# A state-space scan on one core: one product with C for three blocks, carried states by DMA and through the matmul, and the diagonal form of B throughout

## The chip, the cores and the metric

The kernel runs on one core of one Trainium2 chip. The metric is device time in microseconds (us), as the median of several runs. A core has a TensorE (PE; its weight loads are shown on a row of their own, PEld), a VectorE (DVE), a ScalarE (ACT) and a GpSimd (POOL); SyncE (SP) issues most of the transfers here. Each engine works through its own queue in order.

## The reference

Four layers follow each other on eight images of 64 x 64 positions and 192 channels. The change touches only the core of layer 1, a selective scan over L = 4096 positions in four directions k (along rows, along columns, and both backwards), with 384 channels and N = 16 states a channel:

```python
x_hwwh = jnp.stack([x_flat, x_trans], axis=1)
xs = jnp.concatenate([x_hwwh, jnp.flip(x_hwwh, axis=-1)], axis=1)
x_dbl = jnp.einsum('bkdl,kcd->bkcl', xs, x_proj_weight)
dts, Bs, Cs = jnp.split(x_dbl, [R, R + N], axis=2)
dts = jnp.einsum('bkrl,kdr->bkdl', dts, dt_projs_weight)
A = -jnp.exp(A_logs).reshape(4, Din, N)
delta = jax.nn.softplus(dts + dt_projs_bias[None, :, :, None])

def step(h, inp):
    u_l, d_l, B_l, C_l = inp
    dA = jnp.exp(d_l[..., None] * A)
    dBu = d_l[..., None] * B_l[:, :, None, :] * u_l[..., None]
    h = dA * h + dBu
    y = jnp.sum(h * C_l[:, :, None, :], axis=-1)
    return (h, y)
```

So for each channel and each state n: a decay dA that depends on the position, an input d·B·u, the recurrence h = dA·h + dBu, and a sum over n of h·C.

## The kernel before

The program runs layer 0, the input part of layer 1 (projection, convolution), the scan (`layer1_scan`), and a tail with the rest. Each is a stage; the scan's stage does not overlap the others.

The scan is cut into 256 *steps*: image b, direction k, piece p of 512 positions (NJ). For k >= 2 pieces and positions are walked backwards. The first piece of each (b, k) starts from zero, so 7 steps of 8 take over a state from the step before. A step has 16 *groups* (one for each state n, called g over the whole stage), and a group three *blocks* o of 128 channels (j counts blocks; 12288 in all). For one block:

- `ahead(j)`: ACT makes the decay `dA` (128 channels x 512 positions) as an exponential of `dl` times a scalar for each channel. PE makes the input `pd` in PSUM, in four squares of 128x128. The product of step size and input lies in `dut` with positions on partitions; it must be multiplied by B, one number for each position, and turned over. Two forms do this, by turns. For even g (`diagonal`) ACT makes a diagonal matrix `bd` of B (the identity times a scalar for each partition), and PE multiplies `dut` with it (L1009). For odd g ACT multiplies all 384 columns of `dut` by B into `sb`, and PE transposes that (L1011).
- `scan(j)`: DVE runs the recurrence over 512 positions with one instruction (L1044), with the start taken from `st`, the last column of the same state in the step before. POOL multiplies the block with C (`bc`, the row of C on all partitions, brought by a transfer, L993) into `hc` (L1053). After the third block POOL copies the three last columns into `st` (L1055).
- `behind(j)`: PE transposes `hc` in four squares and adds them up over n in PSUM, in `yt` (L942, `add_rows`). After the last n, `take` copies `yt` out with ACT, and a transfer writes it.

`prepare` readies the next step's `dl` and `dut`: transposes (L888, L922), three products (L901), exponentials and logarithms on ACT, and sums and products on DVE. Its pieces are spread over the positions of the current step by the list `at`.

On PE, DVE, ACT and POOL the order is the one written in the program: for each j, in turn, `fetch(g + 2)` (once a group), `ahead(j + 2)`, `scale(g + 2)` (makes `bd` or `sb`), `scan(j)`, `behind(j - 2)`, and what `todo` holds of `prepare`. SP's order is set by a scheduler. Buffers: `dA` 5, `pd` 3, `h` 2 (of three blocks each), `hc` 6 (of one block), `bc` 4, `bd` 10, `sb` 8. All data are f32.

Of the kernel before, what the change touches and what calls it, by code (L numbers as in the profile page):

```python
# [10 lines left out]
AF = mybir.ActivationFunctionType  # L11
ALU = mybir.AluOpType
# [6 lines left out]
DIN = 384  # L19
DP, DT = 128, 3  # L20
NH, HD, NS = 6, 64, 64
N1, R1, K1 = 16, 12, 4
# [3 lines left out]
NJ = 512  # L26
# [3 lines left out]
class Names:  # L30
    n = 0


def mk(pool, shape, tag, **kw):
    Names.n += 1
    return pool.tile(shape, F32, tag=tag, name=f"{tag}_{Names.n}", **kw)
# [795 lines left out]
def layer1_scan(ctx: ExitStack, tc, a, load, ur, ut, xd, yk, cst):  # L832

    nc = tc.nc
    ident = cst[0]
    wp = ctx.enter_context(tc.tile_pool(name="ws1", bufs=1))
    w_dt = load("w_dt", [1 + R1, K1, DIN])
    aneg = load("A_logs", [DP, K1, DT, N1])
    ds = load("Ds", [DP, K1, DT])
    nc.scalar.activation(aneg, aneg, AF.Exp)  # L840
    nc.vector.tensor_scalar(aneg, aneg, -1.0, None, ALU.mult)
    dsum = mk(wp, [DP, DT], "dsum")
    nc.vector.tensor_tensor(dsum, ds[:, 0, :], ds[:, 1, :], ALU.add)
    for k in range(2, K1):
# [5 lines left out]
    pp = ctx.enter_context(tc.tile_pool(name="p1", bufs=2))  # L850
# [17 lines left out]
    steps = []  # L868
# [2 lines left out]
            order = range(NCH) if k < 2 else range(NCH - 1, -1, -1)  # L871
            steps += [(b, k, p, i == 0) for i, p in enumerate(order)]

    def prepare(b, k, p, made):


        def fetch_rows():
            made["xt"] = mk(pp, [128, NB, c], "xt")
            made["dut"] = mk(pp, [128, NB, DIN], "dut")
            for q, v in by_piece(xd[b][:, k, :], k, p):  # L880
                nc.sync.dma_start(made["xt"][q], v)
            for q, v in by_piece(ut[b], k, p):
                nc.sync.dma_start(made["dut"][q], v)

        def turn_xd():
            ps = made["ps"] = mk(psum, [128, NJ], "mm")[:c]
            for t in range(NB):
                nc.tensor.transpose(ps[:, t * 128 : (t + 1) * 128], made["xt"][:, t, :], ident)  # L888

        def turned_xd():  # L890
            xs = made["xs"] = mk(pp, [c, NJ], "xs", bufs=1)
            nc.scalar.copy(xs, made.pop("ps"))
            bcd = made["bcd"] = mk(dram, [N1, NJ], "bcd")
            nc.sync.dma_start(bcd, xs[1 + R1 + N1 :, :])
            made["e"] = mk(pp, [DP, DT, NJ], "e", bufs=1)
            made["dl"] = mk(pp, [DP, DT, NJ], "dl")


        def step_mm(o):
            ps = made["ps", o] = mk(psum, [128, NJ], "mm")  # L900
            nc.tensor.matmul(  # L901
                ps, w_dt[:, k, o * 128 : (o + 1) * 128], made["xs"][0 : 1 + R1, :], start=True, stop=True
            )

        def step_abs(o):
            nc.scalar.activation(made["e"][:, o, :], made["ps", o], AF.Abs)

        def step_exp(o):
            nc.scalar.activation(made["e"][:, o, :], made["e"][:, o, :], AF.Exp, scale=-1.0)

        def step_ln(o):
            nc.scalar.activation(made["e"][:, o, :], made["e"][:, o, :], AF.Ln, bias=1.0)

        def step_add(o):
            nc.vector.scalar_tensor_tensor(  # L915
                made["dl"][:, o, :], made.pop(("ps", o)), 0.0, made["e"][:, o, :], ALU.max, ALU.add
            )

        def turn(t):
            ps = made["pt", t] = mk(psum, [128, NJ], "mm")  # L920
            for o in range(DT):
                nc.tensor.transpose(  # L922
                    ps[:, o * 128 : (o + 1) * 128], made["dl"][:, o, t * 128 : (t + 1) * 128], ident
                )

        def turned(t):
            dut = made["dut"][:, t, :]
            nc.vector.tensor_tensor(dut, made.pop(("pt", t))[:, 0:DIN], dut, ALU.mult)  # L928


        at = [(0, fetch_rows), (8, turn_xd), (9, turned_xd)]
        for o in range(DT):
            at += [(11 + 4 * o, step_mm, o), (12 + 4 * o, step_abs, o), (13 + 4 * o, step_exp, o)]
            at += [(14 + 4 * o, step_ln, o), (16 + 4 * o, step_add, o)]
        for t in range(NB):
            at += [(26 + 3 * t, turn, t), (27 + 3 * t, turned, t)]
        return sorted(at, key=lambda v: v[0])

    def add_rows(yt, src, mat, first, last):
# [27 lines left out]


    PER = N1 * DT
    total = len(steps) * PER  # L970
    ready = [{} for _ in steps]
    brows, decay, turned, states, held, outs, sts = {}, {}, {}, {}, {}, {}, {}

    def diagonal(g):
        return g % 2 == 0

    def scale(g, ts):
        if g >= len(steps) * N1:
            return
        m, n = ready[g // N1], g % N1  # L980
        for t in ts:
            if diagonal(g):
                v, src = mk(sp, [128, 128], "bd", bufs=10), ident
            else:
                v, src = mk(sp, [128, DIN], "sb", bufs=8), m["dut"][:, t, :]
            brows[g, t] = v
            nc.scalar.activation(v, src, AF.Copy, scale=m["xt"][:, t, 1 + R1 + n : 2 + R1 + n])  # L987

    def fetch(g):
        if g < len(steps) * N1:  # L990
# [4 lines left out]
    def ahead(j):  # L995

        if not 0 <= j < total:
            return
        g, o = divmod(j, DT)
        s, n = divmod(g, N1)  # L1000
        k = steps[s][1]
        dA = decay[j] = mk(sp, [DP, NJ], "dA", bufs=5)
        nc.scalar.activation(dA, ready[s]["dl"][:, o, :], AF.Exp, scale=aneg[:, k, o, n : n + 1])  # L1003
        pd = turned[j] = mk(pb, [128, NJ], "pd")
        cols = slice(o * 128, (o + 1) * 128)
        for t in range(NB):
            dst = pd[:, t * 128 : (t + 1) * 128]
            if diagonal(g):
                nc.tensor.matmul(dst, ready[s]["dut"][:, t, cols], brows[g, t], start=True, stop=True)  # L1009
            else:  # L1010
                nc.tensor.transpose(dst, brows[g, t][:, cols], ident)  # L1011

    def behind(j):
        if not 0 <= j < total:
            return
        g, o = divmod(j, DT)
        s, n = divmod(g, N1)
        b, k, p, _ = steps[s]
        if n == 0:
            outs[s, o] = mk(py, [128, NJ], "yt", bufs=DT)  # L1020
        add_rows(outs[s, o], states.pop(j), ident, n == 0, n == N1 - 1)
        if k == 0 and n == 8:
            add_rows(outs[s, o], ready[s]["u", o], dD[:, o, :], False, False)
        if n == N1 - 1:
            late.append((take, s, o, outs.pop((s, o))))

    def scan(j):
        if not 0 <= j < total:
            return
        g, o = divmod(j, DT)  # L1030
        s, n = divmod(g, N1)
        b, k, p, first = steps[s]
        if k == 0 and n == 5:
            v = ready[s]["u", o] = mk(sp, [DP, NJ], "uD", bufs=DT)
            nc.sync.dma_start(v, ur[b][:, o, p * NJ : (p + 1) * NJ])
        if first and n == 0 and o == 0:
            sts[k] = mk(pp, [DP, DT, N1], "st")
        st = sts[k]
        rev = slice(None, None, -1) if k >= 2 else slice(None)
        last = 0 if k >= 2 else NJ - 1  # L1040
        if o == 0:
            states["h"] = mk(sp, [DP, DT, NJ], "h", bufs=2)
        h = states["h"]
        nc.vector.tensor_tensor_scan(  # L1044
            h[:, o, rev],
            decay.pop(j)[:, rev],
            turned.pop(j)[:, rev],
            0.0 if first else st[:, o, n : n + 1],
            ALU.mult,
            ALU.add,  # L1050
        )
        hc = states[j] = mk(sp, [DP, NJ], "hc", bufs=6)
        nc.gpsimd.tensor_tensor(hc, h[:, o, :], held[g], ALU.mult)  # L1053
        if o == DT - 1:
            nc.gpsimd.tensor_copy(st[:, :, n], h[:, :, last])  # L1055

    with every_engine(tc):
        for _, f, *v in prepare(*steps[0][:3], ready[0]):
            f(*v)
            if f.__name__ == "turned_xd":  # L1060
                tc.keep_in_program_order(nc.scalar.preload_act_table_set("natural_log_exp_and_others"))
        fetch(0)
        fetch(1)
        scale(0, range(NB))
        scale(1, range(NB))
        ahead(0)
        ahead(1)
        todo, late = [], []
        for j in range(total + 3):
            g, o = divmod(j, DT)  # L1070
            s, i = divmod(j, PER)
            if i == 5 and s + 1 < len(steps):
                todo = prepare(*steps[s + 1][:3], ready[s + 1])
            if o == 0:
                fetch(g + 2)
            ahead(j + 2)
            scale(g + 2, ((0, 1), (2,), (3,))[o])
            while late:
                f, *v = late.pop(0)
                f(*v)  # L1080
            scan(j)
            behind(j - 2)
            while todo and todo[0][0] <= i - 5:
                _, f, *v = todo.pop(0)
                f(*v)

# [366 lines left out]
```

## Time and profile before

| | |
|---|---|
| runs | 25094.24, 25105.1, 25116.98 us; median 25105.1 |
| profiled execution, span | 25098.0 us |
| layer 0 and input of layer 1 | 0 to 6655 us |
| scan | 6655 to about 22892 us; the tail's first work is mixed into its end |
| instructions: PE, PEld, DVE, ACT, POOL | 156672, 156672, 26682, 40488, 18332 |
| fetches of `bc` | 4096, 256 KB each |
| packets of all transfers | 1506272, mean 93 GB/s |

In the rows of the profile, a group is a line of the program on an engine, then output and inputs by name, shapes, the count, the time in which at least one of them ran, the mean duration of one, and the idle time of that engine just before them with what ended most of it. Matmuls are pipelined, so their durations overlap; how far apart they start is read from the timeline. The stage's busy times of the engines over 40 equal slices, in tenths:

```profile
PE   8999999988899999999999999999999999998999
DVE  6777777766799999999999999999999999998887
ACT  4555555544599999999999999999999999997443
POOL 2322322310399999999999999999999999995110
```

The scan is the long part from the eleventh slice on, where every engine is at nine tenths or more.

### The profile page before, as it was taken

How to read it: one execution, taken by the hardware profiler on the slowest of the kernel's cores; microseconds unless marked ns; L12 is line 12 of the kernel's file. 1: busy time of each engine (PE TensorE's matmuls, PEld its weight loads, DVE VectorE, ACT ScalarE, POOL GpSimd, SP SyncE). 2: the span in 40 equal slices, each digit the busy share in tenths (PEclk: the TensorE clock that was granted, in tenths of full speed). 3: DMA queues.
4: the chain of work that ended last, by engine and by line, in shares of the span. 5: the costliest groups of instructions: out<-in, count | busy, mean ns of one | idle time of the engine just before them, and what ended most of it. 6: DMA issues, size and time to landing. Idle time of an engine off the chain costs nothing.

```text
span 25098.0 us, 445961 instructions
## 1 busy us (share of the span) xinstructions
PE 23784.2 (95%) x156672; PEld 18458.1 (74%) x156672; DVE 22334.3 (89%) x26682; ACT 20190.7 (80%) x40488; POOL 17651.1 (70%) x18332
## 2 busy tenths in 40 slices
PE   8999999988899999999999999999999999998999
PEld 4444444445688888888888888888888888885333
DVE  6777777766799999999999999999999999998887
ACT  4555555544599999999999999999999999997443
POOL 2322322310399999999999999999999999995110
PEclk8888888899999999999999999999999999999999
DMA  1111111123333333333333333333333333335554
GB/s 59 47 43 46 46 47 43 38 70 114 110 100 95 96 101 95 95 103 95 95 101 97 95 99 98 95 97 100 95 95 104 95 95 102 95 95 157 170 175 122
DMA packets 1506272, 2337.12 MB, mean 93 GB/s; under 512 B 249997, under 2 KB 775949, under 8 KB 1504026
## 3 DMA queue, kind: packets, MB, share of 16 engines
q1 hardware_dynamic: 1496858, 2283.42, 31.5%
q8 instruction: 1236, 20.25, 0.3%
q0 software_dynamic: 7168, 25.17, 0.3%
q14 instruction: 1010, 8.27, 0.1%
HBM read 1847.54 MB, written 460.59 MB: 92 GB/s over the span
## 4 chain that ended last, share of the span: by engine, by line
PE 36%; ACT 31%; DVE 13%; POOL 13%; issue 6%; DMA 0%; POOLq 0%; SPq 0%; DVEq 0%; ACTq 0%
ACT dA L1003 13%; POOL hc L1053 11%; ACT sb L987 7%; PE pd L1009 6%; PE yt L942 5%; DVE h L1044 5%; ACT bd L987 4%; PE cv L1282 4%; PE y L592 3%; PE pd L1011 2%; PE mm L901 2%; PE fc L626 2%; PE y L519 1%; PE cv L774 1%; PE tp L564 1%
## 5 line engine op out<-in xcount | busy, mean ns | idle before, releaser
L1053 POOL TENSOR_TENSOR hc<-h,bc 128x512 f32<-128x512 f32 x12288 | 15431.9, 1289 | 475.6 <-DVE h L1044 341.2
L1044 DVE TENSOR_TENSOR_SCAN h<-dA,st,pd 128x512 f32<-128x512 f32 x10752 | 12949.5, 1262 | 530.1 <-PE pd L1009 374.4
L1003 ACT ACTIVATE dA<-dl,A_logs 128x512 f32<-128x512 f32 x12288 | 8817.1, 718 | 47.0 <-DVE h L1044 39.6
L942 PE MATMUL yt<-sq,hc 128*128 128x128 f32 x49152 | 7489.3, 275 | 200.1 <-POOL hc L1053 93.8
L1009 PE MATMUL pd<-bd,dut 128*128 128x128 f32 x49152 | 6581.4, 277 | 254.4 <-DVE h L1044 232.1
L1009 PEld LDWEIGHTS pd<-bd,dut 128*128 128x128 f32 x49152 | 5968.5, 192 | 609.9 <-PE yt L942 342.9
L942 PEld LDWEIGHTS yt<-sq,hc 128*128 128x128 f32 x49152 | 5669.7, 141 | 644.3 <-POOL hc L1053 624.4
L987 ACT ACTIVATE sb<-dut,xt 128x384 f32<-128x384 f32 x8192 | 4779.5, 609 | 1.1 <-DVE dut L928 1.0
L1011 PE MATMUL pd<-sq,sb 128*128 128x128 f32 x24576 | 3739.5, 275 | 8.5 <-DVE h L1044 0.4
L1011 PEld LDWEIGHTS pd<-sq,sb 128*128 128x128 f32 x24576 | 2823.6, 141 | 479.1 <-DVE dl L915 380.8
L987 ACT ACTIVATE bd<-sq,xt 128x128 f32<-128x128 f32 x8192 | 3026.3, 395 | 0.0
L1044 DVE TENSOR_TENSOR_SCAN h<-dA,pd 128x512 f32<-128x512 f32 x1536 | 1770.8, 1204 | 117.0 <-PE pd L1009 67.2
L1143 POOL TENSOR_TENSOR yin<-yin,yin 128x1536 f32<-128x1536 f32 x64 | 233.9, 3655 | 1635.1 <-DMA yin<-y 892.5
L1282 PE MATMUL cv<-x,dgi 96*96 96x512 f32 (+1 forms) x2560 | 1175.0, 595 | 9.3 <-ACT x L1271 9.1
L481 POOL TENSOR_TENSOR xdt<-xb,dtv 128x384 f32<-128x384 f32 x256 | 217.1, 848 | 1186.6 <-ACT xb L475 1186.6
L234 DVE SCALAR_TENSOR_TENSOR x<-xs,cpe_w,x 96x504 f32<-96x504 f32 (+1 forms) x1024 | 886.6, 866 | 31.8 <-ACT x L222 21.7
L784 DVE SCALAR_TENSOR_TENSOR u<-xa,conv_w,u 128x504 f32<-128x504 f32 x1152 | 850.1, 743 | 50.5 <-ACT u L776 12.5
L1282 PEld LDWEIGHTS cv<-x,dgi 96*96 96x96 f32 x2560 | 413.0, 164 | 638.2 <-issue 604.5
L901 PE MATMUL mm<-xs,w_dt 13*128 13x512 f32 x1536 | 863.0, 641 | 1.8 <-DVE dl L915 1.0
L1055 POOL COPY st<-h 128x3 f32<-128x3 f32 x4096 | 825.0, 201 | 0.0
L1303 DVE SCALAR_TENSOR_TENSOR y<-x,wi,y 96x504 f32<-96x504 f32 x1024 | 796.0, 796 | 17.7
L626 PE MATMUL fc<-ff,fc_w 128*96 128x512 f32 x1536 | 791.0, 621 | 2.7 <-DVE xo L629 2.7
(263 smaller groups left out, 26186.7 us busy)
## 6 DMA issues: line engine op xcount, KB each, us to landing
bc<-bcd SPq DMA_DIRECT2D x4096, 256.0 KB
yin<-y SPq DMA_DIRECT2D x256, 768.0 KB
csb<-csd SPq DMA_DIRECT2D x256, 384.0 KB
dut<-ut SPq DMA_DIRECT2D x128, 768.0 KB
y<-ys SPq DMA_DIRECT2D x128, 768.0 KB
dut<-ut SPq DMA_DIRECT2D x256, 384.0 KB
y<-ys SPq DMA_DIRECT2D x256, 384.0 KB
xt<-x1d SPq DMA_DIRECT2D x128, 384.0 KB
```

The costliest lines, as they stand in the source:

```text
L234: nc.vector.scalar_tensor_tensor(d[:, :, w0:w1], s[:, dy : dy + R, w0 + dx : w1 + dx], w[:, ct, tap : tap + 1], d[:, :, w0:w1], ALU.mult, ...
L626: nc.tensor.matmul(ps, f2w[:, o, ct * CP : (ct + 1) * CP], ff[:, o, :], start=o == 0, stop=o == 5)
L784: nc.vector.scalar_tensor_tensor(uv[:, o, :, w0:w1], tv[:, o, dy : dy + R, w0 + dx : w1 + dx], cw[:, o, tap : tap + 1], uv[:, o, :, w0:w1] ...
L901: nc.tensor.matmul(ps, w_dt[:, k, o * 128 : (o + 1) * 128], made["xs"][0 : 1 + R1, :], start=True, stop=True)
L942: nc.tensor.matmul(yt[:, t * 128 : (t + 1) * 128], src[:, t * 128 : (t + 1) * 128], mat, is_transpose=mat is ident, start=first and t == 0 ...
L987: nc.scalar.activation(v, src, AF.Copy, scale=m["xt"][:, t, 1 + R1 + n : 2 + R1 + n])
L1003: nc.scalar.activation(dA, ready[s]["dl"][:, o, :], AF.Exp, scale=aneg[:, k, o, n : n + 1])
L1009: nc.tensor.matmul(dst, ready[s]["dut"][:, t, cols], brows[g, t], start=True, stop=True)
L1011: nc.tensor.transpose(dst, brows[g, t][:, cols], ident)
L1044: nc.vector.tensor_tensor_scan(h[:, o, rev], decay.pop(j)[:, rev], turned.pop(j)[:, rev], 0.0 if first else st[:, o, n : n + 1], ALU.mult, ...
L1053: nc.gpsimd.tensor_tensor(hc, h[:, o, :], held[g], ALU.mult)
L1282: nc.tensor.matmul(pv[:, :, w0:w1], dgi[:, ct, j, :], sv[:, dy : dy + R, w0 + dx : w1 + dx], start=j == 0, stop=j == len(TAPS) - 1, skip_g ...
```

## The change

Five things change, all in `layer1_scan`.

1. The diagonal form is used for every g: `sb` and the transposes of it go, `bd` is made for each group (14 buffers in place of 10).
2. The scan instruction starts from the constant 0.0. The carried state enters by another way: the decay of a piece's first position is made zero, by writing 1e28 into that column of `dl` after all else has read it (`cut`); before that, its true decay is computed as 128x16 values for each block (`first_decay`), and POOL multiplies it with the carried states (`carry`, in two halves) into `v`. PE adds `v` to the first column of `pd` with a product of the identity and one column, on steps that carry a state. (`aneg` is kept below -1e-25 so that the exponent stays large.)
3. The last columns go into `st` by a transfer on SP in place of POOL's copy.
4. POOL multiplies a group's three blocks with C in one instruction, after the third scan.
5. `behind` runs 6 blocks behind the scan in place of 2 (`LAG`), with `h` and `hc` in 3 buffers of three blocks each. `todo` is kept across steps, since the second half of `carry` falls into the next one.

```diff
-    nc.vector.tensor_scalar(aneg, aneg, -1.0, None, ALU.mult)
+    nc.vector.tensor_scalar(aneg, aneg, -1.0, -1e-25, ALU.mult, ALU.min)
...
+        def first_decay(o):
+            if o == 0:
+                made["a0"] = mk(pp, [DP, DT, N1], "a0")
+            nc.scalar.activation(
+                made["a0"][:, o, :], aneg[:, k, o, :], AF.Exp, scale=made["dl"][:, o, edge : edge + 1]
+            )
+
+        def cut():
+            nc.gpsimd.memset(made["dl"][:, :, edge], 1e28)
+
+        def carry(half):
+            if half == 0:
+                made["v"] = mk(pp, [DP, DT, N1], "v")
+            ns = slice(half * N1 // 2, (half + 1) * N1 // 2)
+            nc.gpsimd.tensor_tensor(made["v"][:, :, ns], made["a0"][:, :, ns], sts[k][:, :, ns], ALU.mult)
...
+        at += [(25 + o, first_decay, o) for o in range(DT)] + [(37, cut)]
+        if not first:
+            at += [(38, carry, 0), (49, carry, 1)]
...
         for t in ts:
-            if diagonal(g):
-                v, src = mk(sp, [128, 128], "bd", bufs=10), ident
-            else:
-                v, src = mk(sp, [128, DIN], "sb", bufs=8), m["dut"][:, t, :]
-            brows[g, t] = v
-            nc.scalar.activation(v, src, AF.Copy, scale=m["xt"][:, t, 1 + R1 + n : 2 + R1 + n])
+            v = brows[g, t] = mk(sp, [128, 128], "bd", bufs=14)
+            nc.scalar.activation(v, ident, AF.Copy, scale=m["xt"][:, t, 1 + R1 + n : 2 + R1 + n])
...
         for t in range(NB):
-            dst = pd[:, t * 128 : (t + 1) * 128]
-            if diagonal(g):
-                nc.tensor.matmul(dst, ready[s]["dut"][:, t, cols], brows[g, t], start=True, stop=True)
-            else:
-                nc.tensor.transpose(dst, brows[g, t][:, cols], ident)
+            nc.tensor.matmul(
+                pd[:, t * 128 : (t + 1) * 128],
+                ready[s]["dut"][:, t, cols],
+                brows[g, t],
+                start=t == 0,
+                stop=first,
+                skip_group_check=True,
+            )
+        if not first:
+            edge = NJ - 1 if k >= 2 else 0
+            nc.tensor.matmul(
+                pd[:, edge : edge + 1],
+                ident,
+                ready[s]["v"][:, o, n : n + 1],
+                start=False,
+                stop=True,
+                skip_group_check=True,
+            )
...
-        add_rows(outs[s, o], states.pop(j), ident, n == 0, n == N1 - 1)
+        add_rows(outs[s, o], states[g][:, o, :], ident, n == 0, n == N1 - 1)
...
-            states["h"] = mk(sp, [DP, DT, NJ], "h", bufs=2)
+            states["h"] = mk(sp, [DP, DT, NJ], "h", bufs=3)
...
-            0.0 if first else st[:, o, n : n + 1],
+            0.0,
...
-        hc = states[j] = mk(sp, [DP, NJ], "hc", bufs=6)
-        nc.gpsimd.tensor_tensor(hc, h[:, o, :], held[g], ALU.mult)
         if o == DT - 1:
-            nc.gpsimd.tensor_copy(st[:, :, n], h[:, :, last])
+            nc.sync.dma_start(st[:, :, n], h[:, :, last])
+            hc = states[g] = mk(sp, [DP, DT, NJ], "hc", bufs=3)
+            nc.gpsimd.tensor_tensor(hc, h, held.pop(g).unsqueeze(1).to_broadcast((DP, DT, NJ)), ALU.mult)
...
-        for j in range(total + 3):
+        for j in range(total + LAG + 1):
...
-                todo = prepare(*steps[s + 1][:3], ready[s + 1])
+                todo += [(j + t, *f) for t, *f in prepare(*steps[s + 1], ready[s + 1])]
+                todo.sort(key=lambda v: v[0])
...
-            behind(j - 2)
-            while todo and todo[0][0] <= i - 5:
+            behind(j - LAG)
+            while todo and todo[0][0] <= j:
```

`edge` is 0, or 511 for the directions that run backwards; `LAG` is 2 * DT = 6.

More of the change, by code (lines that the diff above doesn't have):

```diff
@@ L872, in layer1_scan, with prepare @@
             steps += [(b, k, p, i == 0) for i, p in enumerate(order)]
-    def prepare(b, k, p, made):
+    def prepare(b, k, p, first, made):
+        edge = NJ - 1 if k >= 2 else 0
         def fetch_rows():
@@ L969, in layer1_scan @@
     PER = N1 * DT
+    LAG = 2 * DT
     total = len(steps) * PER
@@ L972, in layer1_scan @@
     brows, decay, turned, states, held, outs, sts = {}, {}, {}, {}, {}, {}, {}
-    def diagonal(g):
-        return g % 2 == 0
     def scale(g, ts):
@@ L1005, in ahead @@
         cols = slice(o * 128, (o + 1) * 128)
+        first = steps[s][3]
         for t in range(NB):
-            dst = pd[:, t * 128 : (t + 1) * 128]
-            if diagonal(g):
-                nc.tensor.matmul(dst, ready[s]["dut"][:, t, cols], brows[g, t], start=True, stop=True)
-            else:
-                nc.tensor.transpose(dst, brows[g, t][:, cols], ident)
+            nc.tensor.matmul(
[7 more added lines that the diff above has]
+        if not first:
+            edge = NJ - 1 if k >= 2 else 0
+            nc.tensor.matmul(
[6 more added lines that the diff above has]
+            )
     def behind(j):
@@ L1020, in behind @@
             outs[s, o] = mk(py, [128, NJ], "yt", bufs=DT)
-        add_rows(outs[s, o], states.pop(j), ident, n == 0, n == N1 - 1)
+        add_rows(outs[s, o], states[g][:, o, :], ident, n == 0, n == N1 - 1)
+        if o == DT - 1:
+            del states[g]
         if k == 0 and n == 8:
@@ L1051, in scan @@
         )
-        hc = states[j] = mk(sp, [DP, NJ], "hc", bufs=6)
-        nc.gpsimd.tensor_tensor(hc, h[:, o, :], held[g], ALU.mult)
         if o == DT - 1:
-            nc.gpsimd.tensor_copy(st[:, :, n], h[:, :, last])
+            nc.sync.dma_start(st[:, :, n], h[:, :, last])
+            hc = states[g] = mk(sp, [DP, DT, NJ], "hc", bufs=3)
+            nc.gpsimd.tensor_tensor(hc, h, held.pop(g).unsqueeze(1).to_broadcast((DP, DT, NJ)), ALU.mult)
     with every_engine(tc):
-        for _, f, *v in prepare(*steps[0][:3], ready[0]):
+        for _, f, *v in prepare(*steps[0], ready[0]):
             f(*v)
```

## The prediction

> **What bounds the kernel now.** I read the page's head and engine totals first, then busy times by stage, then the costliest groups, then the order of time inside the stage that the change touches.
>
> ```profile
> span 25098.0 us, 445961 instructions
> PE 23784.2 (95%) x156672; PEld 18458.1 (74%) x156672; DVE 22334.3 (89%) x26682; ACT 20190.7 (80%) x40488; POOL 17651.1 (70%) x18332
> ```
>
> The span is 25098.0 us; the median of the three runs is 25105.1, so about 7 us lie around it. Busy time in the scan's stage (span, then PE, PEld, DVE, ACT, POOL, granted clock, DMA share, GB/s):
>
> ```profile
> 6655.00:22835.00 16180.00, 15710.21 (x129634) 14312.05 (x129635) 15471.80 (x14045) 15792.61 (x31910) 15761.65 (x16326) 1.00 0.35 98
> ```
>
> The reader is to see that four engines stand at 96 to 98% of this stage, at full granted clock: no single one is clearly the bound, and taking work from one helps only until the next stops it. The first PE instruction of the stage starts at 6663.2 us and the last copy out of yt at about 22892, so I count 16229 us for 256 steps, 63.4 us a step (a step is one piece of 512 positions: 16 states n, three blocks o, 48 scans). The rest of the span, 25098 - 16229 = 8869 us, the change does not touch.
>
> The groups that change:
>
> ```profile
> L1053 POOL TENSOR_TENSOR hc<-h,bc 128x512 f32<-128x512 f32 x12288 | 15431.9, 1289 | 475.6 <-DVE h L1044 341.2
> L1044 DVE TENSOR_TENSOR_SCAN h<-dA,st,pd 128x512 f32<-128x512 f32 x10752 | 12949.5, 1262 | 530.1 <-PE pd L1009 374.4
> L942 PE MATMUL yt<-sq,hc 128*128 128x128 f32 x49152 | 7489.3, 275 | 200.1 <-POOL hc L1053 93.8
> L1009 PE MATMUL pd<-bd,dut 128*128 128x128 f32 x49152 | 6581.4, 277 | 254.4 <-DVE h L1044 232.1
> L987 ACT ACTIVATE sb<-dut,xt 128x384 f32<-128x384 f32 x8192 | 4779.5, 609 | 1.1 <-DVE dut L928 1.0
> L1011 PE MATMUL pd<-sq,sb 128*128 128x128 f32 x24576 | 3739.5, 275 | 8.5 <-DVE h L1044 0.4
> L987 ACT ACTIVATE bd<-sq,xt 128x128 f32<-128x128 f32 x8192 | 3026.3, 395 | 0.0
> L1044 DVE TENSOR_TENSOR_SCAN h<-dA,pd 128x512 f32<-128x512 f32 x1536 | 1770.8, 1204 | 117.0 <-PE pd L1009 67.2
> L1143 POOL TENSOR_TENSOR yin<-yin,yin 128x1536 f32<-128x1536 f32 x64 | 233.9, 3655 | 1635.1 <-DMA yin<-y 892.5
> L1055 POOL COPY st<-h 128x3 f32<-128x3 f32 x4096 | 825.0, 201 | 0.0
> ```
>
> The counts hold the key. Half of the 12288 blocks pd are made by L1009, half by L1011, four squares each: 24576 squares by either line. L1011 shows 24576 matmuls, one a square; L1009 shows 49152, two a square: a true f32 product runs as two passes, each with its own weight load, and the f32 transpose as one. The durations of 275 and 277 ns overlap, so they are not the cost; the distances of the starts are. The timeline of PE gives them (start us, us from first start to last end, then the group):
>
> ```profile
> 14003.35 0.60 PE L1011 MATMUL pd<-sq,sb 128*128 128x128 f32 x4
> 14003.79 0.60 PE L942 MATMUL yt<-sq,hc 128*128 128x128 f32 x4
> 14004.23 1.06 PE L1009 MATMUL pd<-bd,dut 128*128 128x128 f32 x8
> 14005.12 0.60 PE L942 MATMUL yt<-sq,hc 128*128 128x128 f32 x4
> 14005.56 1.06 PE L1009 MATMUL pd<-bd,dut 128*128 128x128 f32 x8
> 14006.45 0.60 PE L942 MATMUL yt<-sq,hc 128*128 128x128 f32 x4
> ```
>
> No row shows idle time, so this is PE's own pace: 0.44 us for four transposes (0.110 each), 0.89 us for eight passes (0.111 each). A block by the transposed form costs PE 0.44 + 0.44 = 0.88 us with its yt, one by the diagonal form 1.33. Over the whole trace the distance between neighbouring L1009 passes is 112 ns at the median and nowhere under 108.
>
> PE's work in the scan at this pace: yt 49152 x 0.110 = 5407; L1009 49152 x 0.111 = 5456; L1011 24576 x 0.110 = 2703; the D rows (1536 passes of yt<-dD,uD) 170; preparing a step 16 transposes x 0.110 and three two-pass products of 512 columns at 1.05 (14000.50 to 14001.55 in the timeline) = 4.91 us, x 256 = 1257. Sum 14993 of 16229 us: PE has only 1236 us to give.
>
> **The change part by part.**
>
> *Diagonal form throughout.* ACT gains: 8192 x (609 - 395) ns = 1753 us less. PE loses: 24576 one-pass transposes (2703) become 49152 passes (5456), +2753 us. That is more than twice its slack.
>
> *One-column matmul.* On the 7 pieces of 8 that carry a state, 10752 blocks get a product of the identity with one column; f32 again, so 21504 passes, each with a full 128-column weight load. The trace has no one-column product. The nearest row is layer 0's product of six columns:
>
> ```profile
> 2041.31 1.45 PE L392 MATMUL mm<-w_zdt,hn 96*128 96x6 f32 x12
> ```
>
> Twelve passes in 1.45 us, the last lasting 0.25: (1.45 - 0.25) / 11 = 0.109 us apart, as far as those of 128 columns. So few columns save nothing; the load sets the pace. Inside this run the first two are 30 ns apart (both loads were done while PE waited), the next 141 and 132, the rest 112. Ends: 21504 x 0.030 = 645 and x 0.141 = 3032 us. I take 0.111, since PE here runs in a stream: 2387 us. The Trainium skill ("TensorE: Matmul & The Clock Gate", "Wait — 56ns, not 53.3ns?") states a start-to-start floor near 25 ns for small matmuls; by it this term would be an estimated 540 us and the whole near 27200. The six-column row speaks against it wherever each pass brings its own load.
>
> *PE's new sum*: 5407 + 10912 (98304 x 0.111) + 2387 + 170 + 1257 = 20133 us, far over any other engine. Some 25 us at the stage's two ends stay uncovered (the first yt of before comes 19 us after the stage's first matmul).
>
> *Merged product with C.* Three of 1289 and a copy of 201 (4068 ns a group of three blocks) become one of 128x1536; by the tail's row of that shape 3655 ns. 4096 x 0.41 = 1.7 ms off POOL; at worst, three times 1289, only the copy's 0.8 ms. It waits for all three scans, and yt's transposes of a block are moved from 2 to 6 positions behind it, past the next two groups' pd in PE's order: 4 further positions of 1.5 us cover its 3.7 us. Worth nothing in time, since POOL is then idle a quarter of each step. Without that cover the first transpose would wait about 2.4 us a group.
>
> *Scan with constant start.* 1262 falls to 1204: 10752 x 58 ns = 0.6 ms off DVE, hidden behind PE.
>
> *First decays, cut, carry.* Per step three small ACT exponentials (under bd's 0.395 each, 1.2 us), a memset and two small products on POOL (by the copy's row 0.2 each). Per step ACT has 15793 / 256 = 61.7 - 6.8 + 1.2 = 56 us of 78.6: hidden. The dA of the next piece wait for the cut at position 42, which stands behind a group's product on POOL; its user is emitted four positions later, about 6 us for at most 4 us of POOL. The second carry stands behind the next piece's second product on POOL and is used 18 positions later.
>
> *Last columns by DMA.* 4096 transfers of 128x3 single elements, 384 pieces of 4 bytes. The queue's line for 12000 to 16000 us (packets, MB, share of 16 engines), and SP's longest wait in total (us, times, longest):
>
> ```profile
> q1 hardware_dynamic: 256781, 385.34, 34.1%
> ```
> ```profile
> SPq L993 <- POOL st L1055: 14003.2, 4092, 13.5
> ```
>
> 0.341 x 16 x 4000 / 256781 = 85 ns a packet, most of them 2 KB. Ends for the new packets: zero, and 85 ns each: 384 / 16 x 0.085 = 2.0 us a group. With the present 0.341 x 3.96 = 1.35 us that is 3.4 of 4.9 us, so it fits. SP's row says that its fetches wait almost all the time for buffers; one more issue a group (0.4 to 0.6 us by the rows of xt, also many pieces) is free. Each copy stands on SP behind a bc fetch that waits for the product two groups earlier, and ahead of one whose user is three groups away; the last copy of a piece has some 9 us before the carry. The skill's "DMA: Bandwidth & Descriptors" (Rules for kernel authors) speaks against it: a strided last dimension is one descriptor per element, to be rearranged. The row's price for that count is off the path.
>
> **The sum.** 8869 + 20133 + 25 + 7 = 29034 us, say 29030: 16% slower. By the one-column ends 27290 and 29680.
>
> **The rivals.**
>
> *Other side, faster: the load pace is not PE's limit.* If passes could start closer than in the trace, DVE or POOL would set the step: DVE 15472 - 624 = 14.85 ms, POOL about 4096 x 3.66 = 15.0 ms; 8869 + 15000 + 2% stalls = 24170 us. It needs PE's 176 thousand passes at under 85 ns. The skill's page on TensorE ("Back-to-back issue gap") gives 81 ns for loads and matmuls of 128 columns in a stream, which would carry this rival. Against it: 43000 distances of f32 passes, none below 108 ns, and three blocks in a row at 1.33 us with no wait. 7%.
>
> *Cheap single columns.* PE binds, but loads for one column hide under neighbours: up to 27290. For it: the 30 ns pair. Against: that followed a wait. 8%, for under 28300.
>
> *The small copies become the bound.* If 4-byte pieces took over 150 ns each ((4.9 - 1.35) x 16 / 384), the queue would fall behind, POOL would sit in the carry and PE in the next piece; at 200 ns a group takes 1.35 + 4.8 = 6.15 us: 8869 + 25.2 ms = 34060. For it: 1.57 million packets are added to 1.51 million. Against: the smaller ones should not outlast 2 KB. 5%.
>
> **How the numbers follow.** Forecast 80%; the three rivals 20%. The forecast's own uncertainty is the one-column term (645 to 3032), the preparation (its busy time is 1521 in place of 1257) and stalls at a new rhythm: 28300 to 29800 leaves out somewhat under 2 in 10. A measurement here tells 0.2% from no change. Only the first rival ends below: of its 7%, 6 go to faster and 1 to within 0.2%; slower is 93%.
>
> **What would show it.** Right: the pd product at 98304 passes and the one-column line at 21504, both about 111 ns apart; no idle time before PE in the scan; POOL, DVE and ACT each falling to 70 to 77% of a stage of some 20.1 ms; a step of 78 to 79 us. Wrong: PE rows with idle time released by POOL, DMA or DVE; passes closer than 108 ns; POOL waiting long for st.

## The result, and the profile after

The changed kernel takes 28719.11 us (median of 4 runs, 28717.13 to 28721.18) against 25110.49 before: ratio 1.1439, 95% interval 1.1422 to 1.1455. It is slower by 3.61 ms; 29030 was forecast.

The head of the page, and under it the stage of the scan, from its first transpose to the last one into yt (start and end, length, then PE, PEld, DVE, ACT, POOL, granted clock, DMA share, GB/s):

```profile
span 28715.1 us, 528222 instructions
PE 27858.8 (97%) x202752; PEld 23222.0 (81%) x202752; DVE 22431.8 (78%) x26682; ACT 19002.3 (66%) x41256; POOL 16079.0 (56%) x6748
```
```profile
6670.00:26501.00 19831.00, 19824.27 (x176128) 19109.56 (x176128) 15618.50 (x14080) 14652.92 (x32769) 14251.32 (x4800) 1.00 0.33 80
```

The scan took 16229 us and takes 19831; the rest of the span went from 8869 to 8884. Four engines stood at 96 to 98% before. Now PE has 7 us without work in 19.8 ms, and the others have fallen to 72 to 79%. The groups that answer to those shown of before:

```profile
L1085 POOL TENSOR_TENSOR hc<-h,bc 128x1536 f32<-128x1536 f32 x4096 | 14154.9, 3456 | 5565.4 <-DVE h L1074 4948.0
L1074 DVE TENSOR_TENSOR_SCAN h<-dA,pd 128x512 f32<-128x512 f32 x12288 | 14748.2, 1215 | 3152.3 <-PE pd L1032 1695.8
L1022 PE MATMUL pd<-bd,dut 128*128 128x128 f32 x98304 | 13063.1, 276 | 0.0
L962 PE MATMUL yt<-sq,hc 128*128 128x128 f32 x49152 | 7739.1, 280 | 2.3 <-POOL hc L1085 2.3
L1001 ACT ACTIVATE bd<-sq,xt 128x128 f32<-128x128 f32 x16384 | 5973.7, 389 | 0.0
L1032 PE MATMUL pd<-v,sq 128*128 128x1 f32 x21504 | 3019.5, 210 | 0.0
```

The last column is the idle time before a group: 0.0, 0.0 and 2.3 us on PE, thousands of us on DVE and POOL. Over half of DVE's (1695.8 of 3152.3 us) is ended by the one-column product, the last instruction of a pd. The timeline of PE gives the rhythm:

```profile
16049.93 1.06 PE L1022 MATMUL pd<-bd,dut 128*128 128x128 f32 x8
16050.82 0.28 PE L1032 MATMUL pd<-v,sq 128*128 128x1 f32 x2
16050.96 0.63 PE L962 MATMUL yt<-sq,hc 128*128 128x128 f32 x4
16051.43 1.06 PE L1022 MATMUL pd<-bd,dut 128*128 128x128 f32 x8
```

A block takes 16051.43 - 16049.93 = 1.50 us with a one-column product; on the pieces that carry no state it takes 1.33.

### The profile page after: what moved, and what is told of

Its sections match the earlier page's. It is cut to its first block, busy times and chain, and to the rows that moved or that the text cites. A ratio compares the mean times of both kernels' runs of the same rounds, so it can differ in the third digit from the quotient of the medians.

```text
span 28715.1 us, 528222 instructions
## 1 busy us (share of the span) xinstructions
PE 27858.8 (97%) x202752; PEld 23222.0 (81%) x202752; DVE 22431.8 (78%) x26682; ACT 19002.3 (66%) x41256; POOL 16079.0 (56%) x6748
## 4 chain that ended last, share of the span: by engine, by line
PE 88%; DVE 7%; ACT 3%; POOL 1%; issue 1%; DMA 0%; SPq 0%; ACTq 0%; DVEq 0%; POOLq 0%
PE pd L1022 39%; PE yt L962 21%; PE pd L1032 4%; PE cv L1313 3%; PE mm L902 3%; PE y L592 2%; PE fc L626 1%; PE y L519 1%; PE mm L923 1%; PE cv L774 1%; PE tp L564 1%; DVE x L234 1%; DVE u L784 1%; PE mm L342 1%; PE mm L1232 1%; DVE xs L234 1%
## 5 line engine op out<-in xcount | busy, mean ns | idle before, releaser
L1085 POOL TENSOR_TENSOR hc<-h,bc 128x1536 f32<-128x1536 f32 x4096 | 14154.9, 3456 | 5565.4 <-DVE h L1074 4948.0
L1074 DVE TENSOR_TENSOR_SCAN h<-dA,pd 128x512 f32<-128x512 f32 x12288 | 14748.2, 1215 | 3152.3 <-PE pd L1032 1695.8
L1022 PE MATMUL pd<-bd,dut 128*128 128x128 f32 x98304 | 13063.1, 276 | 0.0
L1022 PEld LDWEIGHTS pd<-bd,dut 128*128 128x128 f32 x98304 | 11942.2, 192 | 580.7 <-issue 366.4
L962 PEld LDWEIGHTS yt<-sq,hc 128*128 128x128 f32 x49152 | 6144.3, 159 | 2.5 <-POOL hc L1085 2.5
L1001 ACT ACTIVATE bd<-sq,xt 128x128 f32<-128x128 f32 x16384 | 5973.7, 389 | 0.0
L1032 PEld LDWEIGHTS pd<-v,sq 128*128 128x128 f32 x21504 | 3265.0, 192 | 0.0
L1032 PE MATMUL pd<-v,sq 128*128 128x1 f32 x21504 | 3019.5, 210 | 0.0
L929 DVE TENSOR_TENSOR dut<-mm,dut 128x384 f32<-128x384 f32 x1024 | 571.0, 558 | 1045.2 <-PE mm L923 1045.0
L907 ACT ACTIVATE e<-mm 128x512 f32<-128x512 f32 x768 | 458.5, 597 | 1250.3 <-PE mm L902 1250.3
```

The costliest lines, as they stand in the source:

```text
L962: nc.tensor.matmul(yt[:, t * 128 : (t + 1) * 128], src[:, t * 128 : (t + 1) * 128], mat, is_transpose=mat is ident, start=first and t == 0 ...
L1001: nc.scalar.activation(v, ident, AF.Copy, scale=m["xt"][:, t, 1 + R1 + n : 2 + R1 + n])
L1022: nc.tensor.matmul(pd[:, t * 128 : (t + 1) * 128], ready[s]["dut"][:, t, cols], brows[g, t], start=t == 0, stop=first, skip_group_check=True,)
L1032: nc.tensor.matmul(pd[:, edge : edge + 1], ident, ready[s]["v"][:, o, n : n + 1], start=False, stop=True, skip_group_check=True,)
L1074: nc.vector.tensor_tensor_scan(h[:, o, rev], decay.pop(j)[:, rev], turned.pop(j)[:, rev], 0.0, ALU.mult, ALU.add,)
L1085: nc.gpsimd.tensor_tensor(hc, h, held.pop(g).unsqueeze(1).to_broadcast((DP, DT, NJ)), ALU.mult)
```

## The experiments

The theory: PE's passes, about 0.11 us apart for 128 columns and not much less for one, set the scan as soon as their sum passes the other engines' work. The rival: the new chain (merged product, small copies, carry) brings waits, and PE's load is only a bystander. Every ratio below is against the kernel before.

### One part alone, and one part undone

**E1, the diagonal form alone**, on the kernel before:

```diff
     def diagonal(g):
-        return g % 2 == 0
+        return True
...
-                v, src = mk(sp, [128, 128], "bd", bufs=10), ident
+                v, src = mk(sp, [128, 128], "bd", bufs=14), ident
```

> The kernel before, with the diagonal form of B for every state and nothing else (14 buffers of bd). Theory (PE's passes, 0.11 us apart each, set the scan once their sum passes the other engines'): PE's sum in the scan is what the changed kernel has there, 19831 us, less the one-column products, 10752 x 0.177 = 1903, so 17930; with the rest of the span, 8880, about 26810 us, half of the change's loss and a bit less. Rival (the loss comes from the new chain of small copies, carry and merged product): no loss from this edit, 24900 to 25200, since ACT even gains 1.75 ms.

Measured: 26821.51 us against 25109.0, ratio 1.0682 (1.0666 to 1.0698). The stage in that run:

```profile
6670.00:24590.00 17920.00, 17916.84 (x154573) 17204.84 (x154572) 16066.61 (x14077) 14393.77 (x31996) 15917.39 (x16378) 1.00 0.30 88
```

PE is busy for 17917 of 17920 us. This part alone costs 1712 us, with none of the new chain in the kernel; the rival can't explain it.

**E2, the transposed form back for every second state** in the changed kernel:

```diff
+    def diagonal(g):
+        return g % 2 == 0
...
             nc.tensor.matmul(
                 pd[:, t * 128 : (t + 1) * 128],
-                ready[s]["dut"][:, t, cols],
-                brows[g, t],
+                ready[s]["dut"][:, t, cols] if diagonal(g) else brows[g, t][:, cols],
+                brows[g, t] if diagonal(g) else ident,
+                is_transpose=not diagonal(g),
```

> The changed kernel with the transposed form back for every second state; merged product, copies by DMA, carry and one-column product stay. Theory: PE loses 49152 passes at 0.112 and gains 24576 transposes at 0.110, 2.79 ms less, 25930 us; PE still without idle time (17040 us of scan, ACT 16400). Rival (the new chain costs): the time stays over 27500, with idle time on PE released by POOL or DMA.

Measured: 25952.35 us, ratio 1.0336 (1.0321 to 1.0352). That is 2767 us less than the changed kernel, where 2790 were expected, with PE still busy for 17015 of 17050 us.

**E3, without the one-column product** (nor cut, carry and first decays; the scan starts from st):

```diff
-            0.0,
+            0.0 if first else st[:, o, n : n + 1],
...
-        if not first:
-            edge = NJ - 1 if k >= 2 else 0
-            nc.tensor.matmul(
-                pd[:, edge : edge + 1],
...
-        at += [(25 + o, first_decay, o) for o in range(DT)] + [(37, cut)]
```

> The changed kernel without one-column product, cut, carry and first decays: the scan starts from st again (which the DMA fills); diagonal form throughout, merged product, copies by DMA stay. Theory: 10752 x 0.177 = 1903 us less, 26810 us; the same time as the kernel before with the diagonal form alone, within 1%, though POOL then has 1.3 ms less to do. Rival (a one-column product costs two full passes, 0.222 us): 2390 us less, 26330. Second rival (the small copies are on the path): the scans wait for st and little is won.

Measured: 26822.9 us, ratio 1.0682 (1.0666 to 1.0698). That is 1896 us less, 0.176 us a product. And it is E1's time to 1.4 us, although POOL is busy for 14169 us here and 15917 there, and the last columns travel by DMA here: while PE binds, the merged product, the copies and the distance to yt together are worth nothing, either way. So the two parts on PE, 1712 us (E1) and 1896 us (E3), make up the whole loss of 3609 us.

**E4, both**: forms by turns as in E2 and the start from st as in E3. Of the change there remain the merged product, the copies by DMA and the distance of 6 blocks.

> Both: forms by turns and start of the scan from st; of the change only the merged product, the copies by DMA and the longer distance to yt stay. Theory: PE's sum falls to some 15140 us, below ACT (about 15800) and DVE (about 15500), so ACT sets the step: 24700 to 24950, a little faster than the kernel before, with POOL near 88% of the scan. Rival (POOL's merged product or the copies bring new waits): slower than 25110.

Measured: 24789.79 us, ratio 0.9873 (0.9856 to 0.9889): 1.3% faster than the kernel before. The stage:

```profile
6670.00:22570.00 15900.00, 15542.36 (x130040) 14397.05 (x130038) 15456.70 (x14079) 15792.12 (x31995) 14191.77 (x4096) 1.00 0.40 100
```

With the two edits on PE gone, ACT is the bound (15792 of 15900), and POOL no longer stands near it.

### Single costs

**E5, a second one-column product**, of zeros, in each block that carries a state:

```diff
         if not first:
             edge = NJ - 1 if k >= 2 else 0
+            nc.tensor.matmul(
+                pd[:, edge : edge + 1], ident, zc, start=False, stop=False, skip_group_check=True
+            )
```

> The changed kernel with a second one-column product in each block that carries a state, of the identity and a column of zeros; the result is the same. Measures what such a product costs in a stream. If each of its passes pays for its whole weight load (0.222 us a product, as predicted), 10752 x 0.222 = 2390 us more, 31110; if it costs what the first one costs by the trace's distances (31 + 112 and 34 at the next transpose, 0.177), 1903 more, 30620; if only the distances of its own pair count (0.143), 1540 more, 30260; if its loads hide under the first one's (0.062), 670 more, 29390.

Measured: 31128.55 us, ratio 1.2397 (1.2378 to 1.2415), 2409 us more: 0.224 us for each added product, the price of two full passes. The timeline (L1035 is the added one):

```profile
16052.05 1.06 PE L1025 MATMUL pd<-bd,dut 128*128 128x128 f32 x8
16052.94 0.28 PE L1035 MATMUL pd<-zc,sq 128*128 128x1 f32 x2
16053.09 0.36 PE L1038 MATMUL pd<-v,sq 128*128 128x1 f32 x2
16053.31 0.64 PE L965 MATMUL yt<-sq,hc 128*128 128x128 f32 x4
16053.78 0.38 PE L926 MATMUL mm<-sq,dl 128*128 128x128 f32 x2
```

From L1035 to L1038 0.15 us, from there to yt 0.22. The starts of the single passes lie 31, 112, 112, 111 and (in yt) 144 ns apart; in the changed kernel 31, 112 and 143. So only the second short pass behind the long ones starts early, and the ones after it are 112 ns apart again; why that one starts early, the trace does not show. In the changed kernel the product adds 31 + 112 ns and 34 more in yt, 177 ns; a further one adds 223.

**E6, yt 2 blocks behind the scan again** in the changed kernel: `LAG = 2` in place of `2 * DT`.

> The changed kernel with yt's transposes 2 blocks behind the scan again in place of 6: takes away the cover of the merged product. The prediction said that the first transpose of a group then waits about 2.4 us: 28719 + 4096 x 2.4 = 38500; from the order on PE and the measured 3.46 us of a product I now get 1.8 us, 36100. PE should show idle time before yt, released by POOL. Rival (POOL runs far enough ahead that the distance does not matter): 28719, no change.

Measured: 37082.75 us (2 runs), ratio 1.4767 (1.474 to 1.4794); 8364 us more, 2.04 us a group. PE's wait and its clock:

```profile
PE yt L962 <- POOL hc L1085: 6216.1, 3835, 4.0
```
```profile
6670.00:34840.00 28170.00, 21535.09 (x176088) 20369.25 (x176086) 15758.08 (x14079) 14888.75 (x32764) 14187.04 (x4799) 0.96 0.23 56
```

6216 / 4096 = 1.5 us a group is the plain wait, near the 1.8 expected. Most of the rest is longer work: PE is busy for 21535 us in place of 19824, 0.4 us a group. The granted clock was 1.00 in the changed kernel's stage and is 0.96 here, and behind some waits the passes are slow, as these rows of the timeline show:

```profile
16056.43 1.10 PE L962 MATMUL yt<-sq,hc 128*128 128x128 f32 x4 [1.94 <-POOL hc L1085]
16057.32 1.92 PE L1022 MATMUL pd<-bd,dut 128*128 128x128 f32 x8
16059.03 0.42 PE L1032 MATMUL pd<-v,sq 128*128 128x1 f32 x2
16059.32 0.91 PE L962 MATMUL yt<-sq,hc 128*128 128x128 f32 x4
16060.06 1.06 PE L1022 MATMUL pd<-bd,dut 128*128 128x128 f32 x8
16060.95 0.28 PE L1032 MATMUL pd<-v,sq 128*128 128x1 f32 x2
```

The eight passes after the wait take 1.71 us (16057.32 to 16059.03), the next eight 0.89. From 16057.3 to 16060.0 us the granted clock was 0.52, and from 16060.0 to 16062.0 it was 1.00: these passes were slow because they ran at half the clock. Not every wait is followed by that: behind the next one in this trace, of 1.24 us, eight passes take 0.89 us again. So the merged product depends on the longer distance; without it this would have been the change's largest cost.

**E7, POOL's copy in place of the DMA** in the changed kernel:

```diff
-            nc.sync.dma_start(st[:, :, n], h[:, :, last])
+            nc.gpsimd.tensor_copy(st[:, :, n], h[:, :, last])
```

> The changed kernel with POOL's copy of the last columns back in place of the DMA. Theory: both stand beside PE's 4.8 us a group, 28719 within 0.2%, packets halved and POOL's busy time up by 0.8 ms. Rival (the small pieces disturb other transfers or the carry): faster by 0.5% or more.

Measured: 28721.32 us, ratio 1.1437 (1.1422 to 1.1453), the changed kernel's time. From 12000 to 18000 us the queue's line, first of this run, then of the changed kernel:

```profile
q1 hardware_dynamic: 314688, 472.64, 28.5%
```
```profile
q1 hardware_dynamic: 811076, 474.75, 33.3%
```

The lines differ by 811076 - 314688 = 496388 packets, 400 for each of the 1241 copies in this stretch (384 pieces and 16 more). (0.333 - 0.285) x 16 x 6000 / 496388 gives about 9 ns for each, not 85.

### What makes the rest faster than the kernel before

**E8, nine states of sixteen in the diagonal form**, on E4: `return g % 2 == 0 or g % 16 == 7`.

> The run with the forms by turns and the start from st, with one more state in sixteen in the diagonal form (9 to 7). There ACT is busy 99% of the scan. Theory: each group moved takes 0.86 us off ACT and lays 1.33 us on PE; 256 groups: ACT 15792 - 219 = 15573, PE about 15140 + 340 = 15480, DVE 15457: 24790 - 220 = 24570, if the engines still run past each other; with three engines within 1% of each other part of it will be lost in waits: 24570 to 24750. Rival (PE's order already binds there): 24790 or more.

Measured: 25061.37 us, ratio 0.9981 (0.9972 to 0.999): 272 us slower than E4. That is the rival's side; the theory gave 24570 to 24750. Busy sums don't show why: ACT fell to 15659 of 16160 us, by 133 us where 219 were computed, and is no longer the bound. The time between the first scans of successive groups does (us, medians, worked out from the starts in the trace):

```
state      4     5     6     7     8     9    10
before  3.76  3.92  5.00  4.11  4.67  4.42  3.99
E4      3.52  3.51  4.18  4.11  4.67  4.63  3.99
E8      3.52  3.52  4.41  5.24  4.73  4.12  3.98
```

State 7 turns into three diagonal blocks at 1.33 us, 3.99 us, and stands where one of the preparation's products of 512 columns lies too. Such a product delays what follows by 1.25 us (in E8's timeline two yt with a pd between start 2.58 us apart around it, 14287.27 to 14289.85, in place of 1.33), so PE needs 5.24 us there, all of the state's time. The added PE work fell into a place where PE had none to give. Whether the ninth state gains anything in a quiet place was not tried.

**E9, POOL's copy in E4** (the edit of E7).

> The run with the forms by turns and the start from st, with POOL's copy of the last columns in place of the DMA. POOL goes from 14190 to about 15010 us of a scan of 15900, still below ACT and DVE. If the copies by DMA are no part of that run's gain: 24790 to 24830. If POOL's share or the later release of st counts: up to 24950. Rival (the 1.57 million small packets cost something): under 24750.

Measured: 24747.21 us, ratio 0.9857 (0.9842 to 0.9871). That is 43 us less than E4 and just inside the rival's range. But E10, which keeps the copies by DMA, takes the same time, so a price of the small packets is not shown.

**E10, three products a group in E4**, copies by DMA and distance kept:

```diff
+        if o == 0:
+            states[g] = mk(sp, [DP, DT, NJ], "hc", bufs=3)
+        nc.gpsimd.tensor_tensor(states[g][:, o, :], h[:, o, :], held[g], ALU.mult)
         if o == DT - 1:
             nc.sync.dma_start(st[:, :, n], h[:, :, last])
-            hc = states[g] = mk(sp, [DP, DT, NJ], "hc", bufs=3)
-            nc.gpsimd.tensor_tensor(hc, h, held.pop(g).unsqueeze(1).to_broadcast((DP, DT, NJ)), ALU.mult)
```

> The same run with the product with C for each block again (three of 1.29 us a group), the copies by DMA and the distance of 6 blocks kept. POOL is then busy about 15430 us. If the gain over the kernel before (320 us) comes from relieving POOL by the merged product: back to 25000 to 25100. If it comes from the longer distance to yt and the copy off POOL: 24790 to 24850.

Measured: 24747.04 us, ratio 0.9856 (0.9839 to 0.9872). That is 43 us below the range on record for the distance, and far from the 25000 for the merged product. So it is not the merged product that wins.

**E11, states 6 and 8 transposed, 7 and 9 diagonal**, in E4: `return g % 16 in (0, 2, 4, 7, 9, 10, 12, 14)`.

> The same run, still half and half, but with the states 6 and 8 transposed and 7 and 9 diagonal. By the periods of the groups, those of states 6 to 9 take 4.2 to 4.7 us in that run where others take 3.5 to 4.0, because there the preparation's products lie on PE (1.1 us each in groups 5, 6 and 8) beside its exponentials on ACT. If PE sets the groups with products: 6 and 8 shorten by up to 0.4 us each, 24790 - 256 x 0.5 = 24660. If ACT sets them: no change, 24790, since the sums of each engine stay.

Measured: 24778.51 us, ratio 0.9869 (0.9855 to 0.9884): no change, as for a stage set by ACT.

**E12, the longer distance alone**: E10 with the edit of E7, that is the kernel before with yt 6 blocks behind the scan, and three buffers of three blocks for h and hc.

> The kernel before with nothing but the longer distance to yt (6 blocks, three buffers of h and of hc): three products and the copy on POOL as before. POOL's work is then about 15260 + 820 = 16080 us, more than ACT's 15790. If the distance alone makes the gain of the last runs: 24750 to 24800. If POOL must also be relieved, by either the merged product or the copy by DMA: POOL sets the step without idle time, 8870 + 16080 + some 50 = 25000, at most 0.5% under the kernel before.

Measured: 24752.67 us against 25101.04, ratio 0.9862 (0.9846 to 0.9879). That is the first of the two outcomes on record, in which the distance alone makes the gain. The sum of 16080 us for POOL, from which the other one (25000) followed, was too high. The stage:

```profile
6670.00:22550.00 15880.00, 15546.45 (x130040) 14399.75 (x130040) 15467.09 (x14121) 15786.40 (x31998) 15747.62 (x16386) 1.00 0.36 100
```

POOL is busy for 15748 us, not 16080: instructions that follow each other on POOL overlap a little. A group of three products and a copy takes 3.85 us (12001.43 to 12005.28 in the timeline), not 3 x 1.29 + 0.20 = 4.07:

```profile
12001.43 3.77 POOL L1079 TENSOR_TENSOR hc<-h,bc 128x512 f32<-128x512 f32 x3
12005.13 0.20 POOL L1081 COPY st<-h 128x3 f32<-128x3 f32 x1
12005.28 3.76 POOL L1079 TENSOR_TENSOR hc<-h,bc 128x512 f32<-128x512 f32 x3
```

What the distance takes away is PE's wait for the product with C. The waits from 8000 to 20000 us of the kernel before have it on top; with it, two more of the list (engine and line, who ended it, us in total, times, longest):

```profile
PEld yt L942 <- POOL hc L1053: 456.7, 1328, 0.5
DVE h L1044 <- PE pd L1009: 327.7, 443, 1.3
POOL hc L1053 <- DVE h L1044: 192.5, 419, 0.9
```

In the whole span the loads for yt wait 644.3 us in the kernel before, and in E12 5.6:

```profile
L959 PEld LDWEIGHTS yt<-sq,hc 128*128 128x128 f32 x49152 | 5776.3, 141 | 5.6 <-POOL hc L1079 5.5
```

The chain of work that ended last has less of POOL in it (shares of the span, first in the kernel before, then in E12):

```profile
PE 36%; ACT 31%; DVE 13%; POOL 13%; issue 6%; DMA 0%; POOLq 0%; SPq 0%; DVEq 0%; ACTq 0%
```
```profile
ACT 47%; PE 40%; DVE 10%; POOL 2%; issue 1%; DMA 0%; SPq 0%; DVEq 0%; ACTq 0%; POOLq 0%
```

I read this as a loop over PE, DVE and POOL with 2 blocks in it: in the kernel before a late product held yt, yt held the next pd in PE's order, pd held the scan, and the scan held the next product. ACT then waited too: it had no work for 387 us of the stage before (16180 less 15793) and for 94 us of E12's (15880 less 15786). The loop itself is argued from the waits; and E12 changes the distance together with the buffers that it needs, so the two are not separated. E4, E9, E10 and E12 all end within 0.2% of each other, with ACT at 99.3% or more of the stage: in these four, ACT is the bound.

## Why the prediction was right

**PE's sum as the bound.** Right: 19824 us of work in 19831, no idle time before PE, and E1, E2 and E3 each move the time by their passes. The forecast of 20133 + 25 us for the scan was 327 too high, because two terms were off and partly cancelled. The one-column product was priced at 0.222 us (2387 in all) and measures 0.177 by the distances (1903 in all) and 0.176 by E3. By the prediction's own sign of being wrong, passes closer than 108 ns, this term failed: the two passes of a product start 31 ns apart. The row of six columns had shown it, and I misread it. Its pair 30 ns apart did not follow a wait of PE; it followed a product of 512 columns, without idle time on PE:

```profile
2040.45 1.02 PE L626 MATMUL fc<-ff,fc_w 128*96 128x512 f32 x2
2041.31 1.45 PE L392 MATMUL mm<-w_zdt,hn 96*128 96x6 f32 x12
```

So the pair stood for a short product behind longer passes, as here, and the distances of 112 ns after it for short ones among their like, as E5's added product shows. The preparation was 157 us too low: 19831 less 12288 blocks at 1.33, 1903 and the D rows' 171 leaves about 1410, 5.5 us a step in place of 4.91. The timeline gives the same: each of its three products of 512 columns adds 1.25 us and not 1.05, since the passes beside it start later too, and 3 x 1.25 + 16 x 0.110 is 5.5. -484 and +157 make -327. For the same reasons a step takes 77.5 us in place of 78 to 79.

**The diagonal form**, +2753: E2 gives 2767. Alone it costs 1712 (E1), because PE first uses up the time it had to spare: 1236 us by my sum, 1079 with the preparation as measured.

**The page's floor of 25 ns** (the Trainium skill, "TensorE: Matmul & The Clock Gate", "Wait — 56ns, not 53.3ns?") has its nearest row here in the 31 ns between the two passes of one product. A whole one-column product never came near it: the term that it put at an estimated 540 us measured 1903.

**The rival on the other side** (passes of 128 columns closer together) has fallen: of 86 thousand neighbouring L1022 passes no two start less than 111 ns apart.

**Merged product**: 3456 in place of 3655 ns, and worth nothing, as forecast, also where PE doesn't bind (E10 against E4). Its cover is needed: a wait of 2.4 us a group without it was forecast, and E6 loses 2.04, of which 1.5 is that wait. The longer distance itself, which I had not priced, is worth 1.4% in the kernel before (E12); I had looked at it only as cover for the new product, though the kernel before showed PE waiting for hc.

**Constant start of the scan**: 1215 in place of 1204 ns, hidden. **First decays, cut, carry**: an exponential takes 0.29 us (0.395 was the upper bound), a carry 0.23 (0.2 assumed); ACT comes to 14653 / 256 = 57.2 us a step against 56 forecast, hidden.

**The small copies**: off the path (E7), nearer to the lower end: about 9 ns a packet. The rule against strided single elements (the skill's "DMA: Bandwidth & Descriptors", "Rules for kernel authors") holds for their count, 1.6 million more packets, and had no price here while PE bound. Where ACT binds, E9 is 43 us faster than E4 with POOL's copy, but the two differ by 0.2% only, their intervals overlap, and E10 has E9's time with the copies by DMA.

## What to carry to other kernels

Before moving work onto TensorE, count its passes and not its columns or its busy time: here an f32 product of up to 128 columns is two passes with a weight load each, an f32 transpose one, and in a stream of its like each takes its 0.11 us, even for one column (E5). Where several engines stand near 97% together, look for the loop of waits that ties them: more distance between producer and consumer, by buffers and order alone, gave 1.4% here, while moving work from ACT to PE gave a loss (E1). And place added work by the engine's load at that position of the step: E8 put it where PE was full.

## What was not expected of the hardware

The second pass of a one-column product starts 31 ns after the first, yet each further such product costs the full 223 ns (E5). Waits of about 2 us on PE cost more than themselves: in E6 the mean granted clock of the stage was 0.96, and eight passes behind a wait were seen to take 1.71 us in place of 0.89, at a granted clock of 0.52. Of the four-byte pieces each took only about 9 ns of a queue's time (E7), though their issue on SP took 0.61 us for a copy.
